# A graph layer with radial bases on one core: bases for four quads at a time, and fewer ties and waits around them

## The chip, the core and the metric

The kernel runs on one core of a Trainium2 chip. A core has five engines that take their instructions from queues of their own: TensorE (PE, with its weight loads shown as PEld), VectorE (DVE), ScalarE (ACT), GpSimd (POOL) and SyncE (SP). Engines wait for each other by semaphores, and DMA transfers run beside them; they are issued from the queues of ACT, POOL and SP. The metric is the device time of one execution in microseconds. Lower is better.

## The reference

A message-passing layer over 12,500 nodes of 128 features and 400,000 edges, which are sorted by destination, and a layer norm behind it:

```python
width = CUTOFF / NUM_RBF * 0.5                     # 10.0, 50
centers = jnp.linspace(0.0, CUTOFF, NUM_RBF)
rbf = jnp.exp(-(distances[:, None] - centers) ** 2 / (2.0 * width * width))
cut = 0.5 * (jnp.cos(jnp.pi * distances / CUTOFF) + 1.0) * (distances <= CUTOFF)
W = (jax.nn.silu(rbf @ fw1 + fb1) @ fw2 + fb2) * cut[:, None]
messages = (h[src] @ pw + pb) * W
agg = jax.ops.segment_sum(messages, dst, num_segments=num_atoms)
return h + (jax.nn.silu(agg @ mw1 + mb1) @ mw2 + mb2)
# then: x = layernorm(x + that)
```

The drawn lengths are spread so far that most edges lie beyond the cutoff of 10, where `cut` is zero and so is the message.

## The kernel before

**Packing.** DVE marks the edges that lie within the cutoff and packs them, in seven chunks, into rows of quads. A quad is 512 packed edges, four columns of 128 (`QT` = 4, `QE` = 512). There are 139 of them in the main loop and its tail (`NL`); the packing of later chunks runs on DVE between the quads of earlier ones. A table `proj` of the projected node features is made by PE and stored in DRAM while the first chunks are packed.

**A quad's work.** POOL issues four gathers (`fetch`, L1099), each an indirect DMA of 128 rows of `proj` into a `quad` or `x` buffer. ACT makes the radial bases from the edges' lengths, which come from DRAM, broadcast over the partitions of the centers, into `d_sb` (`radial`, L1122): a Square (`basis`, L1151) and an Exp (L1155). One basis holds two quads on 102 of the 128 partitions, 51 for each. PE multiplies the bases with the first weights (`first`, L1167, tile `ph`), ACT applies Silu to the products of two quads (`silu`, L1173, tile `s`, 128x1024), and PE multiplies with the second weights into a bank of PSUM (`second`, L1182 for the bias and L1185). DVE multiplies that bank with the gathered rows (`message`, L1201): this is the quad's product `msg`. DVE also writes four one-hot columns for the quad (`place`, L1214, tile `hot`), each of which marks the place of an edge's destination in a window and holds its `cut`. PE multiplies messages with one-hot columns (`sum_up`, L1235, tile `sums`), and DVE adds the sums to the table `aggT` at the window's base (`add`, L1269). The base is an integer in `base_i` that a register load on DVE fetches (`bases_of` L1240, `base_of` L1251), for two quads at a time in most of the loop. `hot` and `msg` have two buffers each up to quad 65 and four from quad 66 (`own`).

**The order.** The loop over quads at L1593 writes all engines' instructions in the order in which the queues take them. At each quad q it issues the product of q, the second layer of q + 2, first layer and Silu of a pair some quads ahead (`octs`), at every fourth quad two bases (four quads), the sums of q, the register load, the columns of q + 1 and the adds of quads two before. From quad 70 on, the node stages (multiplications by `mw1` and `mw2`, layer norm, stores) lie between the quads.

**The gathers' ties.** A gather is not issued as soon as its buffer is free. The program counts DVE's vector instructions in `vectors`, and a table gives the count at which a quad's gathers are due; between its points `pace` interpolates, less one for each of a few earlier quads:

```python
PACE = ((2, 17), (3, 26), (4, 36), (5, 54), (7, 95), (9, 125), (10, 144), (12, 170), (18, 250), ...
        (60, 754), (66, 826), (72, 902), (78, 982), ... (138, 1646), (139, 1666))
```

The gather is written into the program when that count has been reached, and it is tied to (waits for) the DVE instruction of that count (L1093 to L1106).

**The lengths.** `radials` issues a load of 256 KB for each pair of quads, up to three ahead of the bases made. `d_sb` has three buffers. SP issues the first three between its stores of `proj`, and ACT issues the others, each behind an Exp. The arrival is told by a semaphore of each buffer, for which ACT waits before the Square.

Of the kernel before, what the change touches and what calls it, by code (L numbers as in the profile page):

```python
# [21 lines left out]
P = 128  # L22
# [38 lines left out]
PACE = ((2, 17), (3, 26), (4, 36), (5, 54), (7, 95), (9, 125), (10, 144), (12, 170), (18, 250), (24, 324), (30, 373), (36, 458), (42, 544), (48, 612), (54, 691), (60, 754), (66, 826), (72, 902), (78, 982), (84, 1071), (90, 1139), (96, 1218), (102, 1306), (108, 1357), (114, 1414), (120, 1461), (126, 1518), (132, 1580), (138, 1646), (139, 1666))  # L61
VECTORS = ("TensorScalarPtr", "TensorTensor", "CopyPredicated", "TensorReduce", "TensorCopy",
# [29 lines left out]
def kernel(  # L92
# [347 lines left out]
    vectors, queue = [], []  # L440
# [391 lines left out]
    def unpack(c):  # L832
# [88 lines left out]
        def to_places(f, to):  # L921
# [11 lines left out]
            if to is dl:  # L933
                nc.vector.tensor_copy(base_i[:, p0:p0 + np_], tp[0:1, 0, P:P + np_])
            back(t)
# [93 lines left out]
    d_of, rbf_of, ph_of, t_of, s_of, pu_of, got_of, pa_of, hot_of = ({} for _ in range(9))  # L1029


    row_sb = nc.alloc_sbuf_tensor("row_sb", [P, 5, H], F32).ap()
# [10 lines left out]
    own_sb = {}  # L1043
# [3 lines left out]
    d_sb = nc.alloc_sbuf_tensor("d_sb", [P, 3, QE], F32).ap()  # L1047
    d_sem = [tc.alloc_semaphore(f"lengths{i}") for i in range(3)]
# [59 lines left out]
    def quads(o):  # L1108

        return [q for q in (2 * o, 2 * o + 1) if q < NL]  # L1110

    def radial(o, lengths):

        n = math.prod(lengths.shape) // QE
        v = lengths.rearrange("(o h) e -> o h e", o=1)
        if o < 0:
            d = quad_sb[1].rearrange("p j f -> p (j f)")
            nc.gpsimd.dma_start(d, v.to_broadcast([64, 2, QE]))
        else:
            d = d_sb[:, o % 3, :]  # L1120
            eng = nc.sync if o < 3 else nc.scalar
            on_own(eng.dma_start(d, v.to_broadcast([64, 2, QE])), d_sem[o % 3], "lengths")  # L1122
        d_of[o] = d, n

    next_o, based = [0], [0]

    def radials(to):

        while next_o[0] < min(to, based[0] + 3, -(-NL // 2)):
            o = next_o[0]  # L1130
            if not all(chunk_of(q) in stored for q in quads(o)):
                break
            a, b = 4 * o, 2 * quads(o)[-1] + 2
            radial(o, near_d[a:b].rearrange("(h t) e -> h (t e)", t=2))
            next_o[0] += 1
# [4 lines left out]
    def basis(o):  # L1140
        if o not in d_of:
            for q in quads(o):
                while chunk_of(q) not in stored:
                    go_on(todo[0])
            radials(o + 1)
        d, n = d_of.pop(o)
        u = 2 * KR
        rbf = work.tile([P, QE], F32, name="rbf")
        if o >= 0:
            nc.scalar.wait_ge(d_sem[o % 3], 16 * (o // 3 + 1))  # L1150
        a = nc.scalar.activation(rbf[:u], d[:u], AF.Square, bias=rbf_bias[:u], scale=rbf_scale[:u])  # L1151
        if o >= 0:
            tc.declare_no_dep(a.ins, group="lengths", reason="waits on d_sem")
        beside(HIDE[0])
# [96 lines left out]
    def base_of(q, ks=(0, 1)):  # L1251
        for k in ks:
            if k == windows(q):
                break
# [640 lines left out]
```

## Time and profile before

| | |
|---|---|
| three runs | 944.31 us median (941.9 to 945.89) |
| the profiled execution | 950.38 us |
| its span, first to last instruction | 948.8 us |
| mean granted TensorE clock | 0.808 |
| instructions | 11718 |
| gathers issued by POOL | 412 into `quad` from `proj`, 96 into `x`, 48 from `in_x_dram` |
| loads of lengths | 67 on ACT's queue and 3 on SP's, 256 KB each |

This is one profiled execution, some 6 us above the median of the runs. Rows of the timeline have the start, the duration, the engine (with a q behind it for its queue of DMA issues), the line, the operation with its tiles, and in brackets how long the engine sat idle before and what ended it. "remote" and "another core or an unknown queue" are names for a wait whose releaser the profile doesn't see; "issue" is time in which the engine waited for nothing that the profile shows.

### The profile page before, as it was taken

The numbers are of one execution on the slowest core, as the hardware profiler recorded it, in microseconds if no ns is written. First come the engines' busy times: TensorE is split into PE (matmuls) and PEld (weight loads), VectorE is DVE, ScalarE is ACT, GpSimd is POOL, SyncE is SP. The second block draws the span as 40 slices with busy tenths as digits, with TensorE's granted clock in tenths as the row PEclk, the third lists the DMA queues.
The fourth block names the chain that finished last, engine by engine and source line by source line (L and its number), as shares of the span: only waits on it lengthen the run. The fifth ranks groups of instructions, "written<-read, shape, count | busy, mean of one in ns | idle before, by whom it ended". The sixth has DMA issues, their size and how long they took to land.

```text
span 948.8 us, 11718 instructions
## 1 busy us (share of the span) xinstructions
PE 663.7 (70%) x3531; PEld 517.3 (55%) x3531; DVE 565.9 (60%) x1725; ACT 398.0 (42%) x567; POOL 539.2 (57%) x577
## 2 busy tenths in 40 slices
PE   4663737749778867767767786868796675777656
PEld 3552535537556755655555564646575554554444
DVE  8356638745778767767678584646553344443536
ACT  4432622316335443534334433634643542454235
POOL 6346355565556656666666465546565566664661
PEclk8677767778778878888978898769987787778778
DMA  7574421232233223232324122432422342232222
GB/s 243 161 222 154 147 96 34 77 92 81 62 79 120 71 62 82 69 108 77 94 64 136 54 68 67 120 100 67 142 63 63 105 122 67 65 111 81 70 75 74
DMA packets 51295, 91.23 MB, mean 96 GB/s; under 512 B 12928, under 2 KB 18656, under 8 KB 51226
## 3 DMA queue, kind: packets, MB, share of 16 engines
q0 software_dynamic: 18096, 37.30, 15.6%
q1 hardware_dynamic: 22868, 35.09, 11.2%
q10 hardware_dynamic: 10262, 18.05, 6.0%
q8 instruction: 29, 0.48, 0.2%
q14 instruction: 40, 0.33, 0.1%
HBM read 74.59 MB, written 15.79 MB: 95 GB/s over the span
## 4 chain that ended last, share of the span: by engine, by line
PE 42%; another core or an unknown queue 16%; issue 13%; DVE 13%; ACT 10%; DVEq 1%; DMA 1%; ACTq 0%
PE ph L1167 11%; PE bank L1185 9%; PE sums L1235 9%; PE bank L348 5%; DVE hot L1214 3%; PE bank L1182 3%; PE bank L1283 2%; DVE msg L1201 2%; ACT s L1173 2%; ACT rbf L1151 2%; PE bank L1003 1%; PE bank L345 1%; ACT rbf L1155 1%; DVE aggT L1269 1%
## 5 line engine op out<-in xcount | busy, mean ns | idle before, releaser
L1099 POOL DMA_INDIRECT quad<-proj,srci x412 | 391.7, 951 | 274.0 <-issue 86.1
L1185 PEld LDWEIGHTS bank<-fw_sb,s 128*128 128x128 f32 x1112 | 177.1, 225 | 90.2 <-issue 83.6
L1173 ACT ACTIVATE s<-ph 128x1024 f32<-128x1024 f32 x70 | 71.2, 1017 | 335.6 <-PE ph L1167 159.9
L1167 PE MATMUL ph<-rbf,w_sb 102*128 102x512 f32 x278 | 164.1, 719 | 51.7 <-ACT s L1173 35.7
L1185 PE MATMUL bank<-fw_sb,s 128*128 128x128 f32 x1112 | 180.1, 310 | 22.5 <-issue 22.2
L1214 DVE TENSOR_SCALAR hot<-iota_n,dl,cut 128x80 f32<-128x80 f32 (+4 forms) x408 | 111.1, 338 | 107.0 <-PE sums L1235 49.6
L1235 PEld LDWEIGHTS sums<-hot,msg 128*128 128x128 f32 x816 | 121.5, 218 | 61.3 <-issue 40.3
L1235 PE MATMUL sums<-hot,msg 128*128 128x80 f32 (+4 forms) x816 | 122.5, 299 | 17.3 <-DVE msg L1201 10.1
L1099 POOL DMA_INDIRECT x<-proj,srci x96 | 91.4, 952 | 66.4 <-issue 21.3
L1167 PEld LDWEIGHTS ph<-rbf,w_sb 102*128 102x128 f32 x278 | 57.3, 229 | 99.7 <-issue 58.8
L1269 DVE TENSOR_TENSOR aggT<-aggT,sums 128x80 f32 (+4 forms) x209 | 53.9, 258 | 94.1 <-remote 33.8
L1182 PE MATMUL bank<-fb_b,ones_b 96*128 96x512 bf16 x139 | 60.3, 434 | 49.6 <-DVE msg L1201 15.2
L1201 DVE TENSOR_TENSOR msg<-bank,quad 128x512 f32<-128x512 f32 x78 | 53.2, 682 | 46.2 <-remote 32.7
L348 PEld LDWEIGHTS bank<-pw_sb,xT 128*128 128x128 f32 (+1 forms) x292 | 47.2, 232 | 59.0 <-issue 40.3
L1099 POOL DMA_INDIRECT quad<-in_x_dram,srci x48 | 46.3, 965 | 33.9 <-issue 12.6
L1235 PE MATMUL sums<-quad,quad 128*128 128x128 f32 (+3 forms) x296 | 49.4, 309 | 15.8 <-issue 15.2
L1151 ACT ACTIVATE rbf<-d_sb,rbf_bias,rbf_scale 102x512 f32<-102x512 f32 x70 | 56.1, 801 | 0.0
L1235 PEld LDWEIGHTS sums<-quad,quad 128*128 128x128 f32 x296 | 45.0, 225 | 20.1 <-issue 18.8
L348 PE MATMUL bank<-pw_sb,xT 128*128 128x128 f32 (+1 forms) x292 | 48.5, 319 | 6.2 <-ACT xT L1005 5.6
L345 PE MATMUL bank<-pb_b,ones_b 96*128 96x512 bf16 (+2 forms) x38 | 16.8, 443 | 46.4 <-ACT xT L1005 29.0
L1201 DVE TENSOR_TENSOR quad<-bank,quad 128x512 f32<-128x512 f32 (+1 forms) x40 | 25.9, 647 | 38.0 <-DMA quad<-proj,srci 24.2
L1005 ACT COPY xT<-bank 128x512 f32<-128x512 f32 (+1 forms) x37 | 21.3, 580 | 63.5 <-remote 49.0
(278 smaller groups left out, 881.7 us busy)
## 6 DMA issues: line engine op xcount, KB each, us to landing
d_sb<-near_d ACTq DMA_DIRECT2D x67, 256.0 KB
x<-in_x_dram SPq DMA_DIRECT2D x46, 256.0 KB
quad<-proj,srci POOLq DMA_INDIRECT x412
proj<-hp SPq DMA_DIRECT2D x24, 256.0 KB
out_dram<-x SPq DMA_DIRECT2D x22, 256.0 KB
x<-proj,srci POOLq DMA_INDIRECT x96
r_d<-in_edge_weight_dram SPq DMA_DIRECT2D x5, 256.0 KB
r_dst<-in_dst_dram SPq DMA_DIRECT2D x5, 256.0 KB
```

The costliest lines, as they stand in the source:

```text
L345: nc.tensor.matmul(to[:m, a:a + c, :], ones_b[:, :m], bias_b[:, :c, :], start=True, stop=False)
L348: nc.tensor.matmul(to[:m, k, :], lT[:, k * P:k * P + m], w, start=False, stop=(k == a + c - 1))
L1099: g = nc.gpsimd.indirect_dma_start(out=got[:, j, :], out_offset=None, in_=proj if table is None else table, in_offset=bass.IndirectOffsetO ...
L1151: a = nc.scalar.activation(rbf[:u], d[:u], AF.Square, bias=rbf_bias[:u], scale=rbf_scale[:u])
L1167: nc.tensor.matmul(ph[:, h, :], w1_sb[:2 * KR, h, :], rbf[:2 * KR], start=True, stop=True)
L1173: nc.scalar.activation(s[:, :n], ph[:, :n], AF.Silu)
L1182: nc.tensor.matmul(pu, ones_b[:, :P], bias_b["fb2"].rearrange("k j f -> k (j f)"), start=True, stop=False)
L1185: nc.tensor.matmul(pu[:, j * H:(j + 1) * H], s[:, j * P:(j + 1) * P], fw2_sb, start=False, stop=(j == QT - 1))
L1201: nc.vector.tensor_mul(msg[:, a:b, :], pu_of[q].rearrange("p (j f) -> p j f", j=QT)[:, a:b, :], got_of[q][:, a:b, :])
L1214: nc.vector.tensor_scalar(hot[:, j, :wide(q)], iota_n[:, :wide(q)], dl[:, at[0], at[1]], cut[:, at[0], at[1]], op0=OP.is_equal, op1=OP.mult)
L1235: nc.tensor.matmul(pa[:, k * W:k * W + wide(q)], msg[:, j, :], hot[:, j, :wide(q)], start=(j % n == 0), stop=(j % n == n - 1))
L1269: nc.vector.tensor_add(to, to, pa[:, k * W:k * W + wide(q)])
```

## The change

Five edits are made.

1. Square and Exp run once over four quads (102x1024) instead of twice over two. The `rbf` tile is 128x2x512 with one buffer, instead of 128x512 with two. The two quads that share a first layer and a Silu are now 4g and 4g + 2, or 4g + 1 and 4g + 3. One load of 512 KB brings the lengths of four quads; `d_sb` has two buffers of twice the size. Loads are issued up to two groups of four ahead, and only the first on SP.
2. A gather is tied only to products (`message`): to the first product whose count is at least the due count less 6, or to the last product written so far. It is written into the program when the last product's count reaches the due count less 6, or the count reaches the due count plus 6. Gathers ahead of the first product have no tie.
3. The first one-hot column of a quad waits for the last of the sums that read its buffer, and the other three columns for none of them. Before, each of the four waited for its own.
4. A register load brings the bases of up to eight quads, where they lie in one chunk, instead of two.
5. `row_sb`, which this program doesn't use, isn't allocated.

```diff
+HALF = 6
+BASES = 8
...
-        while queue and (queue[0][0] < must or len(vectors) >= pace(*queue[0])):
+        while queue and (queue[0][0] < must or products[-1:] >= [pace(*queue[0]) - HALF]
+                         or len(vectors) >= pace(*queue[0]) + HALF):
             q, j = queue.pop(0)
             fetch(q, js=(j,))
+
+    def tied_to(q, j):
+
+        n = pace(q, j) - HALF
+        return vectors[next((k for k in products if k >= n), products[-1]) - 1]
...
-            if PACE[0][0] <= q < NL:
+            if PACE[0][0] <= q < NL and products:
                 tc.add_manual_dep(
-                    g.ins, vectors[min(pace(q, j), len(vectors)) - 1],
+                    g.ins, tied_to(q, j),
...
-    d_sb = nc.alloc_sbuf_tensor("d_sb", [P, 3, QE], F32).ap()
-    d_sem = [tc.alloc_semaphore(f"lengths{i}") for i in range(3)]
+    d_sb = nc.alloc_sbuf_tensor("d_sb", [P, 2, 2 * QE], F32).ap()
+    d_sem = [tc.alloc_semaphore(f"lengths{i}") for i in range(2)]
...
+    def pair(o):
+
+        return [q for q in (2 * o - o % 2, 2 * o - o % 2 + 2) if q < NL] if o >= 0 else [-2]
...
+    def radial_of(g):
+
+        eng, v = nc.sync if g < 1 else nc.scalar, near_d[8 * g:8 * g + 8]
+        v = v.rearrange("(i h t) e -> i h (t e)", i=1, h=2).to_broadcast([64, 2, 2 * QE])
+        on_own(eng.dma_start(d_sb[:, g % 2], v), d_sem[g % 2], "lengths")
...
+    def of_lengths(d, k):
+
+        u = 2 * KR
+        rbf = work.tile([P, 2, QE], F32, name="rbf", bufs=1)
+        a = nc.scalar.activation(rbf[:u, :k], d[:u, :k], AF.Square, bias=rbf_bias[:u],
+                                 scale=rbf_scale[:u])
+        beside(HIDE[0])
+        nc.scalar.activation(rbf[:u, :k], rbf[:u, :k], AF.Exp, scale=-1.0 / (2.0 * width * width))
+        beside(HIDE[1])
+        return rbf, a
+
+    def basis(g):
...
+        nc.scalar.wait_ge(d_sem[g % 2], 16 * (g // 2 + 1))
+        rbf, a = of_lengths(d_sb[:, g % 2].rearrange("p (o e) -> p o e", o=2), 2)
+        tc.declare_no_dep(a.ins, group="lengths", reason="waits on d_sem")
+        for o in (2 * g, 2 * g + 1):
+            rbf_of[o] = rbf[:, o % 2], len(pair(o))
+        based[0] = g + 1
+        radials(2 * g + 6)
...
+            if id(hot) in read_by:
+                tc.declare_no_dep(i, group="sums", keep=[read_by[id(hot)]] if j == 0 else [],
+                                  reason="a quad's first column waits for the last product")
...
-            bases_of(list(now))
+            ahead = list(now)
+            while (len(ahead) < BASES and ahead[-1] + 1 < min(with_base[0], NL - 7)
+                   and wide(ahead[-1] + 1) == wide(now[0])
+                   and windows(ahead[-1] + 1) == windows(now[0])):
+                ahead.append(ahead[-1] + 1)
+            if any((k, 0) not in bases for k in now):
+                bases_of([k for k in ahead if (k, 0) not in bases])
```

In ACT's queue, at a block of bases in the first third of the program, this stood before (`rbf` is the basis, `d_sb` the lengths, `s` the Silu's result, `xT` and `quad_76` copies of banks):

```order
L1151 ACTIVATE rbf<-d_sb,rbf_bias,rbf_scale 102x512
L1155 ACT_TABLE_LOAD
L1155 ACTIVATE rbf<-rbf 102x512
L1122 DMA d_sb<-near_d 128x1x512
L1151 ACTIVATE rbf<-d_sb,rbf_bias,rbf_scale 102x512
L1155 ACTIVATE rbf<-rbf 102x512
L1122 DMA d_sb<-near_d 128x1x512
L1005 COPY xT<-bank_169 128x512
L1025 COPY quad_76<-bank_169 128x512
L1173 ACT_TABLE_LOAD
```

And this stands in the changed kernel at the same block:

```order
L1154 ACTIVATE rbf<-d_sb,rbf_bias,rbf_scale 102x1024
L1157 ACT_TABLE_LOAD
L1157 ACTIVATE rbf<-rbf 102x1024
L1135 DMA d_sb<-near_d 128x1x1024
L1014 COPY xT<-bank_169 128x512
L1034 COPY quad_76<-bank_169 128x512
L1187 ACT_TABLE_LOAD
```

One Square, one Exp and one issue of a load have gone, and both table loads are still there. In the program as a whole ACT's queue has 330 activations in place of 400 and 40 DMA issues in place of 73.

In POOL's queue, at the gathers of quads 12 to 14 (buffers `quad_85`, `x_86`, `x_87`; DMASW names the semaphores of POOL's own DMA rings, DVE and PE those of the engines), these waits stood before:

```order
L1099 DMA quad_85<-proj,srci 128x128 [waits DMASW3_49,DVE_49]
L1099 DMA quad_85<-proj,srci 128x128 [waits DMASW4_49,DVE_49]
L1099 DMA quad_85<-proj,srci 128x128 [waits DMASW5_49,DVE_49]
L1099 DMA x_86<-proj,srci 128x128 [waits DMASW6_49,DVE_49]
L1099 DMA x_86<-proj,srci 128x128 [waits DMASW7_49,PE_49]
L1099 DMA x_86<-proj,srci 128x128 [waits DMASW0_49]
L1099 DMA x_86<-proj,srci 128x128 [waits DMASW1_49,DVE_49]
L1099 DMA x_87<-proj,srci 128x128 [waits DMASW2_49,DVE_49]
L1099 DMA x_87<-proj,srci 128x128 [waits DMASW3_49,DVE_49]
```

And these stand there in the changed kernel:

```order
L1108 DMA quad_85<-proj,srci 128x128 [waits DMASW3_49]
L1108 DMA quad_85<-proj,srci 128x128 [waits DMASW4_49]
L1108 DMA quad_85<-proj,srci 128x128 [waits DMASW5_49]
L1108 DMA x_86<-proj,srci 128x128 [waits DMASW6_49,PE_49]
L1108 DMA x_86<-proj,srci 128x128 [waits DMASW7_49,PE_49]
L1108 DMA x_86<-proj,srci 128x128 [waits DMASW0_49]
L1108 DMA x_86<-proj,srci 128x128 [waits DMASW1_49]
L1108 DMA x_87<-proj,srci 128x128 [waits DMASW2_49]
L1108 DMA x_87<-proj,srci 128x128 [waits DMASW3_49]
```

The order of the gathers is the same; gathers of one product need no wait of their own behind the first of them. POOL's queue holds 285 semaphore waits of their own in place of 628.

In DVE's queue, at the products of the quads in `quad_80` and `quad_81`, the changed kernel has these rows (`msg` is the product, `hot` the columns, `ISA` the instruction that sets an address from a register):

```order
L1215 TENSOR_TENSOR msg_680<-bank_170,quad_80 128x512 [waits DMASW2_49,DMASW3_49,DMASW1_49,DMASW0_49]
L1268 TENSOR_LOAD base_i [waits DVE_49]
L1229 TENSOR_SCALAR hot_1062<-iota_n,dl,cut 128x112 [waits PE_49]
L1229 TENSOR_SCALAR hot_1062<-iota_n,dl,cut 128x112 x3
L1295 ISA
L1295 TENSOR_TENSOR aggT<-aggT,sums 128x112
L1295 ISA
L1295 TENSOR_TENSOR aggT<-aggT,sums 128x112 [waits DVE_49]
```

And before, some quads on, where a pair of adds follows as well, they read so:

```order
L1201 TENSOR_TENSOR msg_680<-bank_168,x_88 128x512 [waits DMASW3_49,DMASW4_49,DMASW2_49,DMASW1_49]
L1244 TENSOR_LOAD base_i
L1214 TENSOR_SCALAR hot_1073<-iota_n,dl,cut 128x112 [waits PE_49] x4
L1269 ISA
L1269 TENSOR_TENSOR aggT<-aggT,sums 128x112
L1269 ISA
L1269 TENSOR_TENSOR aggT<-aggT,sums 128x112 [waits DVE_49]
```

All four columns waited for PE before, and now the first alone does. Register loads stand at every fourth pair of adds or so: DVE's queue has 30 of them in place of 88. PE's instructions and their order are the same in both kernels.

More of the change, by code (lines that the diff above doesn't have):

```diff
@@ L438, in before_it @@
         return max((m for m in range(q) if place_of(m) == place_of(q)), default=-1)
-    vectors, queue = [], []
+    vectors, queue, products = [], [], []
     def logged(i):
@@ L1143, in basis @@
+    def basis(g):
+        if g == next_g[0]:
+            for q in in_four(g):
                 while chunk_of(q) not in stored:
                     go_on(todo[0])
[L1145 to L1153, printed above, removed]
@@ L1174, in silu @@
         beside(HIDE[2])
-        for h in range(n):
-            s_of[2 * o + h] = s[:, h]
+        for h, q in enumerate(pair(o)[:n]):
+            s_of[q] = s[:, h]
     def second(q):
@@ L1205, in message @@
             got_of.pop(q)
+            products.append(len(vectors))
         gathers()
@@ L1234, in sum_up @@
             k = j // n
-            nc.tensor.matmul(pa[:, k * W:k * W + wide(q)], msg[:, j, :], hot[:, j, :wide(q)],
-                             start=(j % n == 0), stop=(j % n == n - 1))
-    bases = {}
+            i = nc.tensor.matmul(pa[:, k * W:k * W + wide(q)], msg[:, j, :], hot[:, j, :wide(q)],
+                                 start=(j % n == 0), stop=(j % n == n - 1)).ins
+            if not tc.in_control_flow:
+                tc.add_to_no_dep_group("sums", i)
+                read_by[id(hot)] = i
+    bases, with_base = {}, [DIRECT // QT]
     def bases_of(quads_now):
@@ L1564 @@
             next(direct["rest"])
-            for o in (0, 1):
-                basis(o)
+            basis(0)
         if k == FIRST_AT:
@@ L1580 @@
         second(q)
-    for o in (2, 3):
-        basis(o)
+    basis(1)
     next(direct["rest"])
@@ L1615 @@
         if q % 4 == 3:
-            for o in (q // 4 * 2 + 4, q // 4 * 2 + 5):
-                if 2 * o < NL and q < NL - 8:
-                    basis(o)
+            if q < NL - 8:
+                basis(q // 4 + 2)
         sum_up(q, msg)
@@ L1678 @@
     place(q + 1)
-    for o in (octs(q), octs(q + 1)):
-        basis(o)
+    basis(octs(q) // 2)
     add(q)
```

66 lines of the change are left out of this document (27 added, 39 removed).

## The prediction

> **What bounds the kernel now.** I read the page's first section, then the chain that ended last, then the waits of each engine, and last the timeline at single stalls. These rows are the page's: busy time by engine, and the chain by engine and by line.
>
> ```profile
> PE 663.7 (70%) x3531; PEld 517.3 (55%) x3531; DVE 565.9 (60%) x1725; ACT 398.0 (42%) x567; POOL 539.2 (57%) x577
> PE 42%; another core or an unknown queue 16%; issue 13%; DVE 13%; ACT 10%; DVEq 1%; DMA 1%; ACTq 0%
> PE ph L1167 11%; PE bank L1185 9%; PE sums L1235 9%; PE bank L348 5%; DVE hot L1214 3%; PE bank L1182 3%; PE bank L1283 2%; DVE msg L1201 2%; ACT s L1173 2%; ACT rbf L1151 2%; PE bank L1003 1%; PE bank L345 1%; ACT rbf L1155 1%; DVE aggT L1269 1%
> ```
>
> No engine is full. PE, at 70%, carries 42% of the chain. The next largest share, 16%, is "another core or an unknown queue", and one core runs: that is time in which the profile names no releaser. ACT, whose work the change mainly cuts, has 10% of the chain, and the two lines of the bases together 3%. So the change can win little by shortening ACT, unless it also touches the unnamed time. The waits of each engine show how much of that there is:
>
> ```profile
> ACT s L1173 <- PE ph L1167: 159.9, 39, 13.1
> ACT s L1173 <- remote: 109.2, 14, 11.9
> DVE hot L1214 <- PE sums L1235: 49.6, 18, 14.6
> DVE hot L1214 <- remote: 44.9, 18, 5.3
> PE ph L1167 <- ACT rbf L1155: 3.2, 1, 3.2
> POOL quad L1099 <- DVE aggT L1269: 50.0, 29, 8.5
> ```
>
> The numbers are microseconds in total, times, and the longest. ACT waits for PE and not the other way round: PE waited for a basis once, 3.2 us. ACT's silu stood still 14 times for a releaser that the profile can't name, 109.2/14 = 7.8 us each, and DVE's one-hot columns 18 times. These stalls are the part of the span that is not work.
>
> **The bases: one square and one exponential for four quads.** ACT's timeline at one of the 35 basis blocks, and two groups that give the price of a wider instruction:
>
> ```profile
> 710.20 0.80 ACT L1151 ACTIVATE rbf<-d_sb,rbf_bias,rbf_scale 102x512 f32<-102x512 f32 x1
> 711.02 1.28 ACT L1155 ACT_TABLE_LOAD   x1
> 711.04 0.52 ACTq L1122 DMA_DIRECT2D d_sb<-near_d  x1
> 712.31 0.63 ACT L1155 ACTIVATE rbf<-rbf 102x512 f32<-102x512 f32 x1
> 712.85 0.80 ACT L1151 ACTIVATE rbf<-d_sb,rbf_bias,rbf_scale 102x512 f32<-102x512 f32 x1
> 713.68 0.63 ACT L1155 ACTIVATE rbf<-rbf 102x512 f32<-102x512 f32 x1
> 713.68 0.52 ACTq L1122 DMA_DIRECT2D d_sb<-near_d  x1
> 714.33 1.28 ACT L1173 ACT_TABLE_LOAD   x1
> ...
> L1173 ACT ACTIVATE s<-ph 128x1024 f32<-128x1024 f32 x69 | 70.6, 1023 | 332.6 <-PE ph L1167 156.8 <-remote 109.2 <-issue 49.4
> L1151 ACT ACTIVATE rbf<-d_sb,rbf_bias,rbf_scale 102x512 f32<-102x512 f32 x70 | 56.1, 801 | 0.0
> L1155 ACT ACTIVATE rbf<-rbf 102x512 f32<-102x512 f32 x70 | 44.1, 630 | 1.5
> L1285 ACT ACTIVATE zs<-bank 128x512 f32<-128x512 f32 x22 | 13.1, 595 | 54.5 <-PE bank L1283 36.9 <-remote 13.5 <-PE bank L1185 3.0
> ```
>
> A Silu of 1024 elements takes 1023 ns and one of 512 takes 595: 428 ns for 512 more. A Square of 1024 is then about 801 + 428 = 1229 ns, and an Exp 630 + 428 = 1058. In place of two each, a block saves (1602 - 1229) + (1260 - 1058) = 575 ns, and 35 blocks 20.1 us of ACT. The two table loads of a block stay. How much of it is on the path? The chain gives 3% of 948.8 = 28.5 us to the two lines, of 56.1 + 44.1 = 100.2 us that they are busy: 0.28. So **the term is -0.28 x 20.1 = -5.7 us**; by the rounding of the 2% and the 1% it could be -3.8 to -7.6, and with none or all on the path 0 to -20.1. The first pair's product now has to wait for the whole Exp: 710.20 + 1.23 + 1.30 + 1.06 = 713.79 in place of 712.31 + 0.63 = 712.94, so 0.85 us later. PE's own queue hides this, since it waited for a basis only the once quoted above; without the cover it is 35 x 0.85 = 30 us. The rearranged pairs (quads 0 and 2, 1 and 3 of a four) leave each Silu at 1024 elements, and each quad's second product two quads behind it: nothing.
>
> **The loads of lengths.** 70 loads of 256 KB become 35 of 512 KB, issued two groups ahead. An issue takes ACT's queue 0.52 us and lies beside the table load (711.04 in 711.02 to 712.30) or at the end of the block (713.68, over at 714.20, before the 714.33 table load): the row hides it, so nothing is gained. The lengths were there in time, as ACT's square never idled (0.0 in its row). On SP one load of 512 KB takes the place of three; I put that at nothing, with bounds of -1.6 us (three issues of 0.52 us) to +1.6. That fewer and larger transfers could shorten the unnamed stalls is a rival below.
>
> **The waits of the one-hot columns.** The first column now waits for the last of the four sums of the quad that used the buffer before, and the other three for nothing. Before, each column followed its own product. PE's and DVE's timelines at one place:
>
> ```profile
> 430.93 0.57 DVE L1269 TENSOR_TENSOR aggT<-aggT,sums 128x112 f32 x2
> 433.19 0.68 DVE L1201 TENSOR_TENSOR msg<-bank,quad 128x512 f32<-128x512 f32 x1
> 433.80 1.08 DVE L1214 TENSOR_SCALAR hot<-iota_n,dl,cut 128x112 f32<-128x112 f32 x4
> 436.56 0.67 DVE L1201 TENSOR_TENSOR msg<-bank,quad 128x512 f32<-128x512 f32 x1
> 437.15 1.24 DVE L1214 TENSOR_SCALAR hot<-iota_n,dl,cut 128x112 f32<-128x112 f32 x4
> 438.14 0.57 DVE L1269 TENSOR_TENSOR aggT<-aggT,sums 128x112 f32 x2
> ...
> 433.93 1.15 PE L1235 MATMUL sums<-hot,msg 128*128 128x112 f32 x8 [1.72 <-DVE msg L1201]
> ```
>
> The eight entries of a quad's sums span 1.15 us, so the last product ends about 1.15 x 3/4 = 0.86 us after the first. Where DVE really waits there (18 times, 49.6 us), all four columns start up to 0.86 us later and then end 3 x 0.27 us later than before: 18 x 0.81 = 14.6 us as the upper bound, and 0 as the lower (the last product cannot come before the others). Behind them on DVE stand two adds (0.57) and the next product (0.68). PE is the late engine in these waits, and before it needs that product it has the next quad's sums (1.15 us) and a second layer still ahead of it, which hide the delay: I take **nothing**, and without this cover it is the 14.6 us. The three waits that go were for products that end before the one that stays, so nothing is gained either.
>
> **The loads of bases.** 58 fewer register loads on DVE. The iteration at 436.56 has one between the product and the columns (it is one of those in which the adds follow), the one at 433.19 has none: the columns start at 437.15, 0.08 us before the product's 437.23, and at 433.80, 0.07 us before 433.87. I take **nothing**, since the product's 0.67 us hides the load; a load that took all of this and stood on the path would give the other end, 58 x 0.67 = 39 us gained. The Trainium skill, page "DMA: Bandwidth & Descriptors", section "Latency and other measured facts", gives a register load a floor of about 600 ns, which would make this edit the largest gain of the change: an estimate of 58 x 0.6 = 35 us. The trace disagrees in its effect, since columns behind such a load start as early as those without; by the page alone the sum below would be near 904 us.
>
> **The ties of the gathers.** POOL's view at the first long run (first and last rows of a run, with those around it), then what ended with it on ACT, and the same at a later stall:
>
> ```profile
> 104.74 0.94 POOL L1099 DMA_INDIRECT quad<-proj,srci  x1 [3.47 <-DMA proj<-hp]
> ...
> 117.39 0.94 POOL L1099 DMA_INDIRECT x<-proj,srci  x1 [0.30 <-DVE nodes L539]
> 118.63 0.95 POOL L1099 DMA_INDIRECT x<-proj,srci  x1 [0.30 <-issue]
> ...
> 133.62 0.94 POOL L1099 DMA_INDIRECT x<-proj,srci  x1 [0.30 <-issue]
> 147.21 0.95 POOL L1099 DMA_INDIRECT x<-proj,srci  x1 [12.64 <-DVE base_i L934]
> ...
> 120.93 0.69 DVE L1201 TENSOR_TENSOR msg<-bank,quad 128x512 f32<-128x512 f32 x1 [2.03 <-issue]
> 130.49 0.69 DVE L1201 TENSOR_TENSOR msg<-bank,quad 128x512 f32<-128x512 f32 x1 [1.83 <-remote]
> 136.79 0.58 ACT L1005 COPY xT<-bank 128x512 f32<-128x512 f32 x1 [13.56 <-remote]
> ...
> 333.85 0.94 POOL L1099 DMA_INDIRECT quad<-proj,srci  x1 [0.30 <-issue]
> 336.85 1.02 ACT L1173 ACTIVATE s<-ph 128x1024 f32<-128x1024 f32 x1 [7.14 <-remote]
> ```
>
> A gather that waited for DVE (117.39) and one that did not (118.63) have the same 0.30 us ahead of them, so 343 fewer waits on POOL save no time of POOL. What changes is when gathers may start: up to 6 counts of DVE earlier or, where no product falls there, later. Products lie some 12 to 13 counts apart (the table of due counts rises by 76 from quad 66 to 72), so the first product at or behind "due less 6" lies on average at about the due count itself. **Nothing on average** in the flowing part; the bounds are the 50.0 us in 29 waits of POOL for adds above (if they were all on the path, -50), and the slower rival below.
>
> **The sum.** One term is left. Against the profiled execution, 950.38 us with 1.6 us outside the span of 948.8: 950.4 - 5.7 = 944.7. The median of the three runs is 944.31, 6.1 below the profiled run, and the same -5.7 gives **938.6 us**.
>
> **The rivals.** (1) **No change**, 944.3: the chain's 3% is taken up by the engine that is late next. For it: ACT is 42% busy, and its largest wait is for PE's ph (159.9 us), so a Silu that could start earlier often has nothing to work on. Against it: the chain passes through the bases in several places.
>
> (2) **The stalls shrink**, 919: they begin behind a pair of length loads, of which half as many are left. Two stalls of no named releaser, on ACT and on DVE:
>
> ```profile
> 122.61 0.52 ACTq L1122 DMA_DIRECT2D d_sb<-near_d  x1
> ...
> 721.03 0.69 DVE L1201 TENSOR_TENSOR msg<-bank,quad 128x512 f32<-128x512 f32 x1 [8.29 <-remote]
> ```
>
> The 13.56 us of ACT above began at 123.23, 0.6 us behind the load at 122.61; DVE's 8.29 us began at 712.74, 1.7 us behind the load at 711.04. The second load of a pair comes 713.68 - 711.04 = 2.64 us behind the first. If each of the unnamed stalls ended that much earlier, with 16% of 948.8 = 152 us at 7.8 us each, some 19 of them, this is 19 x 2.64 = 50 us; I price it at half, -25. Against it: the bytes are the same.
>
> (3) **Slower, 959**: a stall of PE and ACT lasts as long as POOL's run of gathers. The ACT stall above ended at 136.79, 2.2 us after the run's last gather (133.62 + 0.94 = 134.56); the one at 336.85 ended 2.1 us after 334.79. The mechanism is that gathers back to back hold something that the other engines need. In the changed kernel the 22 gathers of quads 12 to 17, which ran from 104.74 to 147.21, are tied to the first two products (DVE 120.93 and 130.49). Then POOL idles until 120.93 + 0.69 = 121.62 and issues 22 x 1.25 = 27.5 us on end, to 149.1; the stall would end at 151.3 in place of 136.79: +14.5 us, 944.3 + 14.5 = 958.8. It decides where more than (134.56 - 121.62)/1.25 = 10 gathers lie behind that product. Later, each product may release one or two gathers more than before (2 x 1.25 us in each of the 18 unnamed waits of the columns: up to +45 us if each stall stretched with its run). Against it: a stall may have ended the run and not the run the stall, as the gathers are tied to DVE, which stands still too.
>
> That the bases are not in time, so that the change doesn't do what it says, would show as a wait of ACT's square, and costs at most the 30 us above.
>
> **How the numbers follow.** The forecast, -5.7 us, with its own spread of -20 to +3: 0.40, of which 0.25 beyond -0.5% (4.7 us, about what a measurement of this kernel can tell from no change) and 0.15 within. No change 0.15. Shrinking stalls 0.20. Slower 0.25, since two stalls fit it to 0.1 us, but the direction of cause is not shown. Faster 0.45, the same 0.30, slower 0.25. The range runs from somewhat below the second rival, 915, over the third with a little of its later part, 962; the likeliest sign's own is 915 to 939.6.
>
> **What would show it.** Square and Exp of 102x1024 near 1.23 and 1.06 us, 35 each, and the same two table loads: if they are nearer 1.6 and 1.26, the first term is gone. The chain's share of the basis lines should fall by a fifth. PE's wait for rbf should stay near 3 us. The columns' waits for PE sums should come to at most 49.6 + 14.6 us. POOL's gap should be 0.30 us. For the third rival, look at 105 to 155 us: an ACT wait of over 20 us there that ends 2 us behind a run of some 20 gathers. For the second, the "remote" waits of ACT's Silu should fall well below 109.2 us. The forecast is wrong if the chain's unnamed 16% moves by more than a point either way, since one point is 9.5 us, more than all the work removed from the path.

## The result, and the profile after

The changed kernel takes 989.78 us (986.02 to 998.56, 4 runs) against 944.67 us (941.9 to 945.89, 4 runs) for the kernel before: a ratio of 1.0495, 95% interval 1.0417 to 1.0574. It is 45 us slower. The forecast was 938.6 us, with a range up to 962.

These are the busy times and the chain that ended last from the page of the changed kernel (its profiled execution took 986.02 us, its span is 984.4):

```profile
PE 666.5 (68%) x3531; PEld 522.4 (53%) x3531; DVE 562.3 (57%) x1725; ACT 381.0 (39%) x497; POOL 539.3 (55%) x577
PE 24%; issue 15%; DVE 12%; another core or an unknown queue 11%; POOL 9%; ACT 2%; DMA 1%; DVEq 1%; POOLq 0%; ACTq 0%
POOL quad L1108 7%; PE ph L1181 6%; PE bank L1199 6%; PE sums L1256 6%; DVE hot L1229 3%; POOL x L1108 2%; PE bank L350 2%; PE bank L1196 2%; DVE msg L1215 2%; PE bank L1309 1%; DVE aggT L1295 1%; DMA quad<-proj,srci 1%; DVE quad L1229 1%; DVE bank L553 1%
```

The work is as it was: PE within 3 us, DVE 4 us less, ACT 17 us less. POOL's gathers have come onto the chain (7% and 2%), where they did not stand before, and the basis lines have left its list. The engines' shares here add up to 75%, and before to 96%, so the two chains are compared with care. In the waits of the engines (total, times, longest), the lines that answer to those of before read so:

```profile
ACT s L1187 <- remote: 144.2, 17, 14.5
DVE aggT L1295 <- remote: 91.0, 13, 10.9
DVE hot L1229 <- remote: 72.8, 12, 9.0
DVE hot L1229 <- PE sums L1256: 36.1, 12, 16.2
DVE quad L1215 <- DMA quad<-proj,srci: 16.4, 9, 4.3
DVE msg L1215 <- DMA quad<-proj,srci: 15.7, 6, 4.2
POOL quad L1108 <- DVE msg L1215: 105.1, 28, 23.9
```

Beside those that the prediction shows, these lines stood before:

```profile
DVE aggT L1269 <- remote: 33.8, 7, 6.7
DVE quad L1201 <- DMA quad<-proj,srci: 24.2, 10, 4.8
DVE msg L1201 <- DMA quad<-proj,srci: 7.8, 4, 2.3
```

The waits with no named releaser have grown (ACT's Silu from 109.2 to 144.2, the columns from 44.9 to 72.8, the adds from 33.8 to 91.0). The waits for a gather's data have not: 16.4 + 15.7 = 32.1 us, and 24.2 + 7.8 = 32.0 before. So the gathers do not bring their data later than before, and yet all stand still for longer. The two forms that the change made on ACT cost what the first term of the prediction said:

```profile
L1154 ACT ACTIVATE rbf<-d_sb,rbf_bias,rbf_scale 102x1024 f32<-102x1024 f32 x35 | 43.1, 1231 | 0.0
L1157 ACT ACTIVATE rbf<-rbf 102x1024 f32<-102x1024 f32 x35 | 37.0, 1057 | 0.4
```

Where the time goes is read from the start of the same product (DVE) in both traces. Worked out from the timelines:

```
product of quad    before us   changed us   later by
  0                  120.9        122.2        1.2
  4                  169.8        176.6        6.8
 16                  255.7        273.4       17.7
 36                  349.4        372.9       23.6
 64                  494.9        529.5       34.5
100                  696.3        729.7       33.3
the last             939.2        974.1       34.9
```

The whole loss of this pair of traces comes between 121 and 530 us. Its first place is the one that the third rival named. From the timelines of POOL (first and last gather of a run of 22) and of ACT:

```profile
123.14 0.94 POOL L1108 DMA_INDIRECT quad<-proj,srci  x1 [23.93 <-DVE msg L1215]
...
149.39 0.94 POOL L1108 DMA_INDIRECT x<-proj,srci  x1 [0.30 <-issue]
141.53 0.59 ACT L1014 COPY xT<-bank 128x512 f32<-128x512 f32 x1 [10.18 <-remote]
154.14 0.59 ACT L1034 COPY quad<-bank 128x512 f32<-128x512 f32 x1 [12.02 <-remote]
```

POOL waited 23.93 us for the first product and then issued 22 gathers on end, to 150.33. ACT stood still twice, 22 us in all. The first stall ended inside the run, at 141.53, and the second 3.8 us behind it. (One stall of 13.56 us stood here before.)

### The profile page after: what moved, and what is told of

Same layout as the page of the kernel before. It is cut to its first block, busy times and chain, and to the rows that moved or that the text cites. A ratio compares the mean times of both kernels' runs of the same rounds, so it can differ in the third digit from the quotient of the medians.

```text
span 984.4 us, 11231 instructions
## 1 busy us (share of the span) xinstructions
PE 666.5 (68%) x3531; PEld 522.4 (53%) x3531; DVE 562.3 (57%) x1725; ACT 381.0 (39%) x497; POOL 539.3 (55%) x577
## 4 chain that ended last, share of the span: by engine, by line
PE 24%; issue 15%; DVE 12%; another core or an unknown queue 11%; POOL 9%; ACT 2%; DMA 1%; DVEq 1%; POOLq 0%; ACTq 0%
POOL quad L1108 7%; PE ph L1181 6%; PE bank L1199 6%; PE sums L1256 6%; DVE hot L1229 3%; POOL x L1108 2%; PE bank L350 2%; PE bank L1196 2%; DVE msg L1215 2%; PE bank L1309 1%; DVE aggT L1295 1%; DMA quad<-proj,srci 1%; DVE quad L1229 1%; DVE bank L553 1%
## 5 line engine op out<-in xcount | busy, mean ns | idle before, releaser
L1199 PEld LDWEIGHTS bank<-fw_sb,s 128*128 128x128 f32 x1112 | 183.4, 232 | 114.5 <-issue 97.5
L1187 ACT ACTIVATE s<-ph 128x1024 f32<-128x1024 f32 x70 | 71.3, 1018 | 347.0 <-remote 144.2
L1199 PE MATMUL bank<-fw_sb,s 128*128 128x128 f32 x1112 | 185.6, 318 | 19.0 <-issue 15.8
L1229 DVE TENSOR_SCALAR hot<-iota_n,dl,cut 128x80 f32<-128x80 f32 (+4 forms) x408 | 108.5, 337 | 128.6 <-remote 72.8
L1181 PE MATMUL ph<-rbf,w_sb 102*128 102x512 f32 x278 | 156.5, 691 | 14.8 <-issue 8.8
L1256 PE MATMUL sums<-hot,msg 128*128 128x80 f32 (+4 forms) x816 | 123.1, 297 | 28.7 <-DVE msg L1215 15.1
L1196 PE MATMUL bank<-fb_b,ones_b 96*128 96x512 bf16 x139 | 62.4, 449 | 78.0 <-issue 26.2
L350 PEld LDWEIGHTS bank<-pw_sb,xT 128*128 128x128 f32 (+1 forms) x292 | 47.2, 232 | 45.7 <-issue 32.1
L350 PEld LDWEIGHTS bank<-mw_sb,zs 128*128 128x128 f32 x192 | 31.6, 237 | 32.9 <-ACT zs L1311 17.9
L350 PE MATMUL bank<-mw_sb,zs 128*128 128x128 f32 x192 | 32.5, 322 | 20.0 <-ACT zs L1311 15.5
L1187 ACT ACT_TABLE_LOAD x35 | 44.9, 1283 | 0.6
L1157 ACT ACT_TABLE_LOAD x35 | 44.9, 1283 | 0.6
```

What stands on the lines that cost most here:

```text
L350: nc.tensor.matmul(to[:m, k, :], lT[:, k * P:k * P + m], w, start=False, stop=(k == a + c - 1))
L1157: nc.scalar.activation(rbf[:u, :k], rbf[:u, :k], AF.Exp, scale=-1.0 / (2.0 * width * width))
L1181: nc.tensor.matmul(ph[:, h, :], w1_sb[:2 * KR, h, :], rbf[:2 * KR], start=True, stop=True)
L1187: nc.scalar.activation(s[:, :n], ph[:, :n], AF.Silu)
L1196: nc.tensor.matmul(pu, ones_b[:, :P], bias_b["fb2"].rearrange("k j f -> k (j f)"), start=True, stop=False)
L1199: nc.tensor.matmul(pu[:, j * H:(j + 1) * H], s[:, j * P:(j + 1) * P], fw2_sb, start=False, stop=(j == QT - 1))
```

## The experiments

Runs of one group share a chip and the runs of the kernel before on it, whose medians came to 953 to 957 us for the first four groups, on three chips, so ratios are compared, not times.

**Which edit.** Each side of the ties, and of the bases, apart. The old ties in the changed kernel are these lines, and the other kernels move the same lines (or those of the bases) the other way:

```diff
-        while queue and (queue[0][0] < must or products[-1:] >= [pace(*queue[0]) - HALF]
-                         or len(vectors) >= pace(*queue[0]) + HALF):
+        while queue and (queue[0][0] < must or len(vectors) >= pace(*queue[0])):
...
-                    g.ins, tied_to(q, j),
+                    g.ins, vectors[min(pace(q, j), len(vectors)) - 1],
```

The changed kernel with the old ties:

> The changed kernel with the gathers' ties of before (each gather tied to the DVE instruction of its due count), all else as changed. Theory T (the 45 us come from tying gathers to products alone: POOL waits longer and then runs longer, and PE stands still with it): 936 to 946 us. Rival B (they come from the bases: one 512 KB load, one basis for four quads, the first pair's product later): 980 to 990 us. Rival H (from the columns that wait for the last of the sums): 980 to 990 us.

Measured: 954.64 us, ratio 0.9923 (0.9871 to 0.9976).

The kernel before with the new ties alone:

> The kernel before with the new ties of the gathers alone. T: 980 to 995 us. B and H: 941 to 947 us, no change.

Measured: 1013.52 us, ratio 1.0627 (1.0544 to 1.0710).

The changed kernel with the old bases, loads of lengths and pairs:

> The changed kernel with the bases, loads of lengths and pairs of before. T: 985 to 1000 us, since the 6 us that the bases were to win are missing. B: 941 to 947 us. H: 985 to 1000 us.

Measured: 1014.48 us, ratio 1.0566 (1.0475 to 1.0657).

The new bases, loads of lengths and pairs alone:

> The kernel before with the new bases, loads of lengths and pairs alone. T: 936 to 941 us, the forecast term of -5.7. B: 980 to 990 us. H: 936 to 941 us.

Measured: 948.70 us, ratio 0.9935 (0.9900 to 0.9970), which is -6.2 us of 955.73. The loss is that of the ties, and B and H fall. The bases win what they were to win. The columns and the register loads together make no difference that these intervals can show (0.9923 with them, 0.9935 without). They were not run apart, so a small gain of one and a small loss of the other could hide each other.

**Where, and what about the ties.** First the new ties for a part of the quads, by a condition on `q`, here and in `gathers`:

```diff
-            if PACE[0][0] <= q < NL:
+            if PACE[0][0] <= q < NL and (products or not (q < 18)):
                 tc.add_manual_dep(
-                    g.ins, vectors[min(pace(q, j), len(vectors)) - 1],
+                    g.ins, tied_to(q, j) if q < 18 else vectors[min(pace(q, j), len(vectors)) - 1],
```

> The kernel before with the new ties for quads 2 to 17 only. Theory E (the third rival's first place: 22 gathers behind the first two products, one long stall): the whole loss is here, +45 to +60 us against before. Theory L (a loop: where DVE stands still, POOL used to stop after a gather or two and now runs on, and PE stands still with it, at many places): +5 to +15 us.

Measured: 968.05 us, ratio 1.0118 (1.0071 to 1.0164), +11 us. This is what L expected, and E falls.

With `q >= 70` as the condition:

> The kernel before with the new ties from quad 70 on only. The traces of before and of the changed kernel keep their distance from quad 64 on (35 us at the product of quad 64 and 35 at the last), so both L and E expect within 0.7% of before. Theory G (any tie to products costs, since gathers come in lumps of a quad): half of the loss, +25 to +30 us.

Measured: 971.61 us, ratio 1.0150 (1.0086 to 1.0214), +14 us, which none of the three theories had foreseen: this part costs too, though the two traces had kept their distance there. Of the 60 us of the ties alone, 34 are left for quads 18 to 69 by subtraction, if the parts add up; this part was not run alone.

The same ties, but to the last column of a quad, not its product (the line `products.append(len(vectors))` moves from `message` to the end of `place`):

> The kernel before with the new ties, but to the last one-hot column that stands behind each product instead of the product itself: as coarse (one tie a quad), but held back while DVE waits at the columns, which is where it waits most in the first half. L: at most a third of the loss, 0 to +20 us against before. G: the same loss as with products, +50 to +60 us.

Measured: 1000.51 us, ratio 1.0407 (1.0331 to 1.0484), +39 us. Two thirds of the loss is there without any tie to a product: L's +20 is missed, and G is nearer.

The old fine ties, each 6 counts earlier (`return n - 6 - ...` in `pace`):

> The kernel before with its own fine ties, each 6 counts of DVE earlier. Theory A (what costs is that gathers may start earlier, whatever they are tied to): +30 to +60 us. L: +5 to +25 us, since POOL is still held back gather by gather when DVE stands still, but a little later each time. G: no change.

Measured: 962.24 us, ratio 1.0021 (0.9970 to 1.0071). That gathers may start earlier costs nothing that can be seen, as G expected. Theory A falls; the +5 us at the lower end of L lies just inside the interval.

So lumps were tried by themselves. The kernel before, with `j` rounded at the head of `pace`, so that two gathers, or all four of a quad, are due at the same count:

```diff
     def pace(q, j):
 
+        j = j // 2 * 2 + 0.5
+
```

> The kernel before with its own ties, but two gathers share one: the mean of their due counts. Theory G (what costs is that gathers are released in lumps, whatever DVE instruction releases them): +8 to +25 us against before. Theory Q (lumps are harmless, and it is the product as the releaser that costs): within 0.7%.

Measured: 968.60 us, ratio 1.0140 (1.0059 to 1.0221).

With `j = 1.5`:

> The same with all four gathers of a quad on one tie, at the quad's mean due count. G: +25 to +50 us, as with the ties to the last column (+39). Q: within 0.7% of before.

Measured: 986.34 us, ratio 1.0301 (1.0204 to 1.0399). The loss grows with the lump while the releasing instructions stay those of before, as G expected, and Q falls: lumps are not harmless. But +29 us is half of the 60 us that ties to products cost, so lumps alone do not show where the other half comes from.

**Whether the loads of lengths take part.** The stalls of before often began behind such loads (the prediction's second rival), so they were left out, and with them the waits for them. In the changed kernel:

```diff
-        on_own(eng.dma_start(d_sb[:, g % 2], v), d_sem[g % 2], "lengths")
+        if g < 2:
+            on_own(eng.dma_start(d_sb[:, g % 2], v), d_sem[g % 2], "lengths")
```

> The kernel before without the loads of lengths on ACT's queue: all but the first three loads are left out, and the bases of later quads are made from the lengths of the first ones. Theory S (the standstills of PE come from a load of lengths and a run of gathers together): 60 to 150 us faster than before. Theory N (gathers alone, or something else): within 20 us of before.

Measured: 950.47 us, ratio 0.9953 (0.9908 to 0.9997).

> The changed kernel without the loads of lengths behind the first two: the bases of later quads are made from the lengths of the first ones. S: within 15 us of the kernel before without loads. N: 35 to 55 us slower than that one.

Measured: 1004.93 us, ratio 1.0444 (1.0318 to 1.0571). N is right: without the loads the kernel before gains 0.5% and the changed one is still 4.4% slower than the kernel before, so the second rival's mechanism falls.

**Long runs and stalls.** This table is worked out from the rows of each trace: a run is a row of gathers with under 0.45 us between them, and the share is that of the time in which PE neither multiplied nor loaded weights.

```
                     runs  gathers each  longest   PE idle, by the time since the run began
                                                   0 to 7.5 us   7.5 to 10    beyond 10
before                106      5.3          19         13%          24%       69% of 133 us
lumps of 2             89      6.3          19         14%          19%       65% of 128 us
lumps of 4             72      7.8          20         16%          26%       56% of 133 us
changed                74      7.6          22         15%          27%       60% of 162 us
```

In every one of these traces PE works as usual for the first 7.5 us of a run (six gathers), and mostly stands still beyond 10 us (eight gathers). But the table does not carry the loss: the time in which PE idles beyond 10 us is 92, 83, 74 and 97 us by it, and the runs of over eight gathers are 27, 28, 21 and 25. The two halves of the kernel tell more. They are parted at the product of quad 64; "beyond" is the time beyond 10 us of a run, all in us:

```
                        first product to quad 64       quad 64 to the last product
                        length   beyond   PE idle      length   beyond   PE idle
before                  374.0      39       109        444.3      71       112
lumps of 4              386.7      35       109        471.7      79       130
ties to last column     389.1      35       120        479.5      82       139
ties alone              413.7      70       148        457.7      64       124
changed                 407.3      67       138        444.6      72       113
```

With ties to products, the time beyond 10 us of a run nearly doubles in the first half, and PE's idle time grows with it: 29 of the 33 us that the changed kernel loses there. Lumps of four and ties to the last column lose mostly in the second half and leave the first half's long runs as they were. So they show that lumps cost, and not that the changed kernel loses in the same way; what products add in the first half over columns, which release just as coarsely, was not run apart. In the lumps of four PE also works longer, 683.5 us against 663.7, at a granted clock of 0.790 against 0.808. Whether the lumps bring this about is open.

What such a stall looks like is seen on PE in the kernel before, ahead of the ACT row at 336.85 that the prediction quotes:

```profile
329.52 1.88 PE L1167 MATMUL ph<-rbf,w_sb 102*128 102x512 f32 x4
331.24 1.02 PE L1235 MATMUL sums<-hot,msg 128*128 128x80 f32 x8
332.09 0.38 PE L1182 MATMUL bank<-fb_b,ones_b 96*128 96x512 bf16 x1
332.31 1.05 PE L1185 MATMUL bank<-fw_sb,s 128*128 128x128 f32 x8
337.93 1.22 PE L1167 MATMUL ph<-rbf,w_sb 102*128 102x512 f32 x1 [4.56 <-ACT s L1173]
```

By PE's records the four `ph` products were over at 331.40, and the Silu that needs them began at 336.85. In between the trace has no update of PE's semaphore (it keeps 508 of 602 of them), and then five within 0.17 us, at 336.83 to 337.00. What ACT waited for was PE's signal, which came 2 us behind the last gather of the run (333.85 to 334.79). That PE's own record lies so far back may be why the profile names no releaser.

A long run could still be the effect of the stall, not its cause. So runs were broken up. Every sixth gather waits for the landing of the one before it:

```diff
+            issued.append(g.ins.name)
+            if len(issued) % 6 == 0 and not tc.in_control_flow:
+                tc.add_manual_dep(g.ins, issued[-2], mybir.DependencyInfo(
+                    mybir.DependencyClass.Sync, mybir.DependencyReason.DATA))
```

> The changed kernel, every sixth gather waiting for the landing of the one before it (a pause of about 1.3 us; 94 of them). Theory R (a long run holds PE up): 10 to 30 us faster than the changed kernel's 1.05 of before, so 1.02 to 1.04. Theory K (a late POOL is the bound, and pauses make it later): 1.06 to 1.12.

Measured: 928.72 us, ratio 0.9714 (0.9651 to 0.9778).

> The kernel before with the same pauses. R: 0.97 to 1.00 of before. K: 1.02 to 1.08, since 94 x 1.3 = 122 us of POOL's time go, of some 400 us in which it does nothing.

Measured: 944.90 us, ratio 0.9852 (0.9791 to 0.9914).

For the longer pause, the same at every eighth gather, with four writes of a scratch tile ahead of it on POOL:

```diff
+            if len(issued) % 8 == 7 and not tc.in_control_flow:
+                for _ in range(4):
+                    nc.gpsimd.iota(idle_sb, pattern=[[1, 500]], base=0, channel_multiplier=0)
```

> The kernel before with a longer pause ahead of every eighth gather (four writes of a scratch tile on POOL, about 2.3 us, 70 of them, 160 us of POOL). R: 0.96 to 1.00. K: 1.03 to 1.10.

Measured: 925.90 us, ratio 0.9671 (0.9608 to 0.9734).

> The changed kernel with the longer pause ahead of every eighth gather. R: 1.00 to 1.04 of before. K: 1.07 to 1.14.

Measured: 931.61 us, ratio 0.9734 (0.9681 to 0.9787). R's direction holds in all four, and K falls; for the changed kernel both times lie below the range that R gave. Pauses that take POOL's time make both kernels faster than the kernel before, and the loss of the changed kernel is gone: it is 16 us faster than the kernel before with the same pauses at every sixth gather, and 6 us slower with those at every eighth. Busy times and waits of the changed kernel with a pause at every sixth gather, and a pause on POOL's timeline:

```profile
PE 660.3 (71%) x3531; PEld 510.8 (55%) x3531; DVE 563.0 (61%) x1725; ACT 382.5 (41%) x497; POOL 539.8 (58%) x577
...
DVE msg L1221 <- DMA quad<-proj,srci: 106.4, 35, 7.0
POOL quad L1108 <- DMA quad<-proj,srci: 103.1, 46, 5.6
DVE quad L1221 <- DMA quad<-proj,srci: 91.8, 28, 9.0
ACT s L1193 <- remote: 3.8, 1, 3.8
...
338.01 0.94 POOL L1108 DMA_INDIRECT quad<-proj,srci  x1 [0.30 <-DVE aggT L1301]
340.83 0.94 POOL L1108 DMA_INDIRECT quad<-proj,srci  x1 [1.88 <-DMA quad<-proj,srci]
```

The Silu's unnamed wait fell from 144.2 to 3.8 us. In its place DVE waits for gathers, 106.4 + 91.8 us where it was 32: POOL is late now, as theory K said of pauses, and this costs less than the stalls did. (That one wait is no measure of the loss by itself: with the old ties in the changed kernel it was 168.1 us, in an execution of 962.22 us, at a ratio of 0.9923.)

**The last group, on another chip.** One run asks if a pause at every twelfth gather, which lets runs of 9 to 12 come back, brings the stalls back, and one has the old ties with pauses.

> The changed kernel with the longer pause ahead of every twelfth gather instead of every eighth. If the length of a run decides, and PE is held up beyond about 8 gathers: 0.99 to 1.03 of before, since runs of 9 to 12 are possible again. If any pause helps, whatever the length of the runs: 0.97 to 0.98, as with every eighth.

Measured: 857.72 us, ratio 1.1654 (1.1627 to 1.1681).

> The changed kernel with the ties of before and the longer pause ahead of every eighth gather. If the bases keep their 0.6% beside the pauses: 0.955 to 0.963 of before (the kernel before with these pauses had 0.967). If POOL is the bound then, and ACT's time is hidden: 0.964 to 0.972.

Measured: 919.72 us, ratio 1.2514 (1.2478 to 1.2551). Neither run can decide between its two expectations, for the kernel before took 735.66 us on this chip (734.36 to 736.83, 7 runs), with a granted clock of 0.906 to 0.921, where it had taken 953 to 957 on three others, at 0.79 to 0.82. From the page and the waits of the changed kernel with a pause at every twelfth gather, and the group of the pauses in it, and behind that the same group of the other kernel:

```profile
POOL 33%; issue 15%; DVE 13%; DMA 11%; PE 6%; DVEq 1%; POOLq 0%; ACT 0%; ACTq 0%
...
DVE msg L1225 <- DMA quad<-proj,srci: 92.8, 32, 5.2
DVE quad L1225 <- DMA quad<-proj,srci: 80.2, 27, 6.7
L1110 POOL IOTA idle_sb<- 128x500 int32 x184 | 102.7, 558 | 9.8
```

```profile
L1109 POOL IOTA idle_sb<- 128x500 int32 x276 | 152.4, 552 | 14.7
```

Here no wait of any engine is "remote", and the runs of up to 13 gathers did not stop PE: it idled 25% of the time in the first 7.5 us of a run and 23% beyond 10. POOL leads the chain. The kernels have 184/4 = 46 and 276/4 = 69 pauses, and the 23 more cost 919.72 - 857.72 = 62 us, 2.7 us each. Without any, this leads to 857.72 - 46 x 2.7 = 734 us, an estimate which takes the two ties as equal here, and which is near the time of the kernel before. On this chip a pause costs its whole length, as K had it. The changed kernel itself was not run on it, and the kernel before left no trace there.

With a pause at every eighth gather the chips nearly agree, though these are three kernels: 919.72 us here (old ties, new bases), and 925.90 (the kernel before) and 931.61 (the changed one) on the chip where the kernel before without pauses took 955.56. The granted clocks are alike too, 0.831 to 0.844 here and 0.822 to 0.847 there. But there ACT's Silu still waited 52.7 and 48.6 us for a releaser with no name, and here not at all, so a higher granted clock alone is not what spares this chip the stalls.

## Why the prediction was wrong

**The bases: right.** 1229 and 1058 ns were expected for Square and Exp, and 1231 and 1057 came. The share of the chain turned 20.1 us of ACT into -5.7, and alone they made -6.2 (-9.6 to -2.9), with their loads and pairs.

**The loads of lengths, the columns and the register loads: right, as nothing.** Together with the bases they are at 0.9923, and the bases alone at 0.9935. The columns' waits for PE sums came to 36.1 us, where up to 64.2 had been allowed. The floor of about 600 ns for a register load, from the Trainium skill's page "DMA: Bandwidth & Descriptors", section "Latency and other measured facts", led to an estimate of 35 us, 3.7% of the time; the runs don't show such a gain for the loads and the columns together.

**The ties of the gathers: this step failed.** The prediction put them at "nothing on average", since the first product at or behind "due less 6" lies on average at the due count. The run with all ties 6 counts earlier shows that the mean hardly matters (1.0021). What the step left out is the spread: one release for four gathers or more, in place of one for each. Alone the ties cost 6.3%, some 60 us of 956. Lumps of four at the due counts of before cost 3.0%. In the first half of the kernel, ties to products bring longer runs and with them 29 us more of idle PE; why products do more there than columns is open.

**The third rival had the mechanism, and was priced too low.** It said that a stall lasts as long as POOL's run of gathers. For its first place it gave a run from 121.6 to 149.1 us and +14.5 us; the run went from 123.1 to 150.3, and the ties up to quad 17 cost +11 us. The price is near, though the stall came as two, and the first of them ended inside the run. Its other part, "one or two gathers more" at every later stall and up to +45 us, was not in its time of 959, and only a little of it in the range up to 962. This part was most of the loss: 60 - 11 = 49 us of the ties alone, if the parts add up. It did not come as more long runs, but as longer ones: 162 us of the changed trace lie beyond 10 us of a run, and 133 before.

**The second rival fell.** That stalls began behind a load of lengths was no sign of a cause: without the loads the time hardly changes (0.9953).

**The prediction's own sign of being wrong came, with an odd direction.** The chain's unnamed share moved by more than a point, from 16% to 11%: down, while ACT's and DVE's waits with no named releaser grew. With a quarter of the changed kernel's chain left unassigned, that share could not tell which way the stalls went.

**"No engine is full" misled.** 556 gathers at 1.25 us are 695 us of POOL. On the chip whose two traces have no such stall the kernel before ends at 735.66, so POOL is probably close to the bound there: an estimate, since that kernel left no trace on it. Where the stalls occur, this is hidden behind them.

## What to carry to other kernels

When many small transfers are tied to another engine's progress, the spread of the releases counts, not only their mean: release them one by one, and look at how long the runs become. If waits end without a named releaser, set their ends beside the ends of another engine's runs; if they agree, break up the runs by pauses to see which is the cause. And do not take a tuning against such a stall as won for good before it has been timed on several chips: pauses gave up to 3% on one and took 17 to 25% on another.

## What the runs showed of the hardware

- Beyond some eight indirect gathers in a row (1.25 us each), PE idles 56 to 69% of the time in the four traces of the first table, and 13 to 16% in the first 7.5 us of a run. Where the trace was read closely, PE's signals came late by several microseconds, 2 to 4 us behind the last gather; one stall ended inside its run. With the runs broken up, on a chip where the kernel before takes 955.56 us, the Silu's unnamed wait falls to 3.8 us. What in the chip holds the signals back was not found.
- The same kernel takes 735.66 us on one chip and 953 to 957 on three others, with nothing else changed. With a pause at every eighth gather three kernels of these edits come within some 1% of each other, 919.72 on the first chip against 925.90 and 931.61 on another. What sets the chips apart is open. How long a run has to be for a stall is open too, since the pause at every twelfth gather was timed on the chip without stalls alone.
